# A hand-written order for TensorE and VectorE in the first attention, matmuls of ones before it, and an earlier small load

## The chip, the cores and the metric

One core of one Trainium2 chip runs the whole kernel. The metric is the device time of one execution in microseconds; the profile's span, from the first to the last instruction, is a little shorter. Engines are named as the profile names them: PE (matmul), PEld (its weight loads), DVE (vector), ACT (scalar), POOL (GpSimd), SP (the queue that issues most transfers).

## The reference

The input is x (2 sequences of 1024 rows, 256 wide) and a context (2 x 77 x 192). Everything is float32. Four layers follow each other, each with a residual:

```
x = x + attn0(LN(x), ctx)     # 16 heads of 16, 77 keys, softmax per head
x = x + ffn0(LN(x))           # t + relu(t w1 + b1) w2 + b2, then LN(gamma, beta); t = LN(x)
x = x + attn1(LN(x), ctx)     # one head of 256, own layer norms
x = x + ffn1(LN(x))           # row s uses the matrix W[idx[s]] of 8; idx = argmax(pe @ sign(sigs))
```

In ffn0 the router's weights are replaced by one for expert 0, so only w1[0] and w2[0] count. idx depends on the position alone and is computed from the tile signatures, a table of 8 x 32.

## The kernel before, in words

The 2048 rows are cut into 8 chunks (c) of 256 rows; a chunk has two blocks (b = 2c and 2c + 1) of 128 rows. Each chunk passes attention0, ffn0, attention1 and then to_slots, which sorts its rows by tile into a buffer in device memory, from which block() reads them sorted, or, for the last chunk, by_every_tile.

The code is written as Python generators. Each piece of work is begun with a place, a number on a common scale, and each `yield` gives the place of its next step; `run` (line 159) takes steps from a heap by place and emits their instructions. So places give a program order. From this a planner makes the order on each engine: by default it may advance an instruction whose inputs it expects to be ready. With `manual_schedule(engines=...)` the instructions emitted inside keep their program order on the engines named. Before the change this holds for DVE in steps with a place below 0 (line 874); everything after it (line 875) and all other engines are left to the planner:

```
    run(0, {mybir.EngineType.DVE})
    run(math.inf)
```

Semaphores and buffers are assigned by the framework. Each engine takes its own instructions in the order that results.

The work around the change:
- Loads (lines 93 to 117). SP issues most of them, ACT issues x_0 and wq. Those after `late = True` (line 103) are issued after the first chunk's xT copy ("a0"). The signatures sigT are the 19th load, near the end, on SP.
- first_context (299): the context is transposed (ps_cxT, line 268, copied by DVE, 275) and projected to keys (ps_k, 288); DVE writes them masked by head into kbd (305).
- attention0 (568): moments on DVE (187, 189) and POOL (196, 197); normed on ACT (227), transposed on PE (254), copied by ACT (257); queries ps_q (580) with bias on ACT (585).
- attention0_block (591): scores sc (599), 16 matmuls into the one buffer of four PSUM banks; for each half g a row maximum mx (608) and a subtraction (610) on DVE and an exponential on ACT (614); sums per head (617), reciprocal (621), spread over the head's width on ACT (623: sme); 12 transposes in three banks (634), each copied by ACT (635): ten of the probabilities and, in the third bank, two of sme; weighted values ps_o (643), times the reciprocal on DVE (650: oT); output ps_y (656), added to x by DVE (657). One generator writes these in that order, with pauses before the sums, the transposes, ps_o and ps_y.
- values (327): ps_v (332), copied by ACT (336), spread by five products (341), masked by DVE into vbd (321); then transfers to v_rows for sequence 1.
- row_of_biases (362): bvb on DVE (365), ps_bv (368), added to a row (369), which POOL adds to x (566).
- ffn0 (659): moments, normed, transposed, eight hidden tiles of 128 in four steps (ps_h, 676), two outputs (ps_eo, 688).
- choices (452) computes idx and reads sigT in DVE (455, 456); second_context (375) prepares attention1.

All other matmul results share four PSUM banks (tag "bank").

Of the kernel before, what the change touches and what calls it, by code (L numbers as in the profile page):

```python
# [35 lines left out]
P = 128  # L36
# [27 lines left out]
def tile_blocks(ctx: ExitStack, tc: tile.TileContext, a: dict, out: bass.AP):  # L64
# [12 lines left out]
    def load(name, shape, src, eng=nc.sync, tag=None, bufs=None):  # L77

        if tag is None:
            t = const.tile(shape, F32, tag=name, name=name)  # L80
        else:
            t = work.tile(shape, F32, tag=tag, name=name, bufs=bufs)
        i = eng.dma_start(t, src)
        if late:
            loads.append(i.ins)
        return t
# [9 lines left out]
    cols = load("cols", [P, N_COL], a["cols"])  # L96
    wk = load("wk", [CK, 2, D], rows_of(a["wk"], CK), tag="blk", bufs=6)
    wq = load("wq", [P, KC, D], rows_of(a["wq"]), nc.scalar)
    wv = load("wv", [CK, 2, D], rows_of(a["wv"], CK), tag="blk", bufs=6)
    xs.append(load("x_1", [P, NI, D], x_in[1]))  # L100
    wo = load("wo", [P, KC, D], rows_of(a["wo"]))
# [8 lines left out]
    wv1 = load("wv1", [CK, 2, D], rows_of(a["wv1"], CK), tag="both", bufs=4)  # L110
    wqT = load("wqT", [P, KC, D], rows_of(a["wqT"]), tag="both", bufs=4)
    wo1 = load("wo1", [P, KC, D], rows_of(a["wo1"]), tag="both", bufs=4)
    sigT = load("sigT", [NP, NT], a["sigT"])
    peT = [
        load(f"peT_{s}", [NP, S // 2], a["peT"][:, s * S // 2 : (s + 1) * S // 2], tag="blk", bufs=6)
        for s in range(2)
# [2 lines left out]
    def col(i, p=P):  # L119
        return cols[:p, i : i + 1]  # L120
# [171 lines left out]
        return ps  # L292

    kbd = const.tile([P, B, KC, 2, L], F32, tag="kbd", name="kbd")
    first = {}
# [29 lines left out]
    def values():  # L327
        v = work.tile([L, B, D], F32, tag="tb", name="v")
        ps = bank("ps_v").rearrange("p (e d) -> p e d", e=B)
        for e in range(B):  # L330
            for k in range(2):
                nc.tensor.matmul(
                    ps[:L, e, :], first["cxT"][:, k, e * L : (e + 1) * L], wv[:, k, :],
                    start=k == 0, stop=k == 1,
                )
        nc.scalar.copy(v, ps[:L])
        for c in range(NK):
            yield
            ps = bank(f"ps_v_{c}")
            n0 = c * P % L  # L340
            nc.tensor.matmul(
                ps[:, :D], repeat[:, n0 : n0 + P], v[:, 0, :], start=True, stop=True
            )
            masked(0, c, ps[:, :D], nc.vector)
        yield
        none = work.tile([NK * P - G8, D], F32, tag="yT", name="none", bufs=3)
        nc.gpsimd.memset(none, 0.0)
        nc.sync.dma_start(v_rows[G8:, :], none)
        nc.sync.dma_start(
            v_rows[:G8, :].rearrange("(h l) d -> l h d", l=L),  # L350
            v[:, 1, :].unsqueeze(1).to_broadcast([L, 8, D]),
        )
# [7 lines left out]


    def row_of_biases():
        bvb = work.tile([P, KC, P], F32, tag="oT", name="bvb")
        for k in range(KC):
            nc.vector.tensor_scalar(bvb[:, k, :], ones, col(C_BV + k), None, ALU.mult)
        ps = bank("ps_bv")
        for k in range(KC):
            nc.tensor.matmul(ps[:, :D], bvb[:, k, :], wo[:, k, :], start=k == 0, stop=k == KC - 1)
        nc.vector.tensor_tensor(rows[:, R_BO, :], ps[:, :D], rows[:, R_BO, :], ALU.add)
# [198 lines left out]
    def attention0(c, x):  # L568
        e = c * CH // S
        m = moments(x, NI, f"a{c}")  # L570
        yield 2 * c - 1.8
        n = normed(x, NI, D, f"a{c}", m, act=True)
        yield 2 * c - 1.4
        xT = transposed(n, f"a{c}")
        yield 2 * c - 0.7
        qT = work.tile([P, KC, CH], F32, tag="qT", name=f"qT_{c}")
        ps = bank(f"ps_q_{c}").rearrange("p (g t) -> p g t", g=KC)
        for g in range(KC):
            for k in range(KC):
                nc.tensor.matmul(  # L580
                    ps[:, g, :], wq[:, k, g * P : (g + 1) * P], xT[:, k, :],
                    start=k == 0, stop=k == KC - 1,
                )
        for g in range(KC):
            nc.scalar.activation(qT[:, g, :], ps[:, g, :], AF.Identity, bias=col(C_BQ + g))
        for i in range(NI):
            begin(2 * c + i, attention0_block(c, i, e, x, qT))
        yield 2 * c + 1.2
        with_row(x, x, R_BO)

    def attention0_block(c, i, e, x, qT):
        b = c * NI + i
        pr = prs[b % len(prs)]
        sm = work.tile([P, KC * 8], F32, tag="sm", name=f"sm_{b}", bufs=3)
        sc = ps2.tile([P, 4, 512], F32, tag="sc", name=f"sc_{b}")
        for g in range(KC):
            for j in range(4):
                quarter = slice(j * 32, j * 32 + 32)
                nc.tensor.matmul(  # L599
                    sc[:, j, g * 2 * L : (g + 1) * 2 * L],  # L600
                    qT[quarter, g, i * P : (i + 1) * P],
                    kbd[quarter, e, g].rearrange("p h l -> p (h l)"),
                    start=True, stop=True,
                )
        for g in range(KC):
            scv = sc[:, :, g * 2 * L : (g + 1) * 2 * L].rearrange("p j (h l) -> p j h l", l=L)
            mx = work.tile([P, 4, 2], F32, tag="mx", name=f"mx_{b}_{g}")
            nc.vector.tensor_reduce(mx, scv, AX.X, ALU.max)  # L608
            p8 = pr[:, g, :G8]
            nc.vector.tensor_tensor(  # L610
                p8.rearrange("p (j h l) -> p j h l", j=4, l=L), scv,
                mx.unsqueeze(3).to_broadcast([P, 4, 2, L]), ALU.subtract,
            )
            nc.scalar.activation(p8, p8, AF.Exp, scale=1.0 / math.sqrt(HD))  # L614
        yield b + 0.5
        for g in range(KC):
            nc.vector.tensor_reduce(  # L617
                sm[:, g * 8 : g * 8 + 8], pr[:, g, :G8].rearrange("p (h l) -> p h l", l=L),
                AX.X, ALU.add,
            )  # L620
        nc.vector.reciprocal(sm, sm)
        sme = work.tile([P, KC, 8, HD], F32, tag="sme", name=f"sme_{b}")
        nc.scalar.copy(
            sme, sm.rearrange("p (g h) -> p g h", g=KC).unsqueeze(3).to_broadcast([P, KC, 8, HD])
        )
        yield b + 0.7

        pT = work.tile([P, 3, 4, P], F32, tag="pT", name=f"pT_{b}")
        srcs = [pr[:, g, n * P : (n + 1) * P] for g in range(KC) for n in range(NK)]
        srcs += [sme[:, g].rearrange("p h d -> p (h d)") for g in range(KC)]  # L630
        for n in range(3):
            ps = bank(f"ps_pT_{b}_{n}")
            for j in range(4):
                nc.tensor.transpose(ps[:, j * P : (j + 1) * P], srcs[4 * n + j], ident)  # L634
            nc.scalar.copy(pT[:, n].rearrange("p j t -> p (j t)"), ps)  # L635
        pTs = pT.rearrange("p n j t -> p (n j) t")
        yield b + 1.1
        ps = bank(f"ps_o_{b}")
        for g in range(KC):
            for m in range(4):  # L640
                n0 = 2 * L * m // P
                for n in (n0, n0 + 1):
                    nc.tensor.matmul(  # L643
                        ps[32 * m : 32 * m + 32, g * P : (g + 1) * P],
                        vbd[:, e, n, g, 32 * m : 32 * m + 32],
                        pTs[:, g * NK + n, :],
                        start=n == n0, stop=n > n0,
                    )
        oT = work.tile([P, KC, P], F32, tag="oT", name=f"oT_{b}")
        nc.vector.tensor_tensor(  # L650
            oT, ps[:, : KC * P].rearrange("p (g t) -> p g t", g=KC), pTs[:, KC * NK :, :], ALU.mult
        )
        yield b + 1.5
        ps = bank(f"ps_y_{b}")
        for g in range(KC):
            nc.tensor.matmul(ps[:, :D], oT[:, g, :], wo[:, g, :], start=g == 0, stop=g == KC - 1)  # L656
        nc.vector.tensor_tensor(x[:, i, :], ps[:, :D], x[:, i, :], ALU.add)

    def ffn0(c, x):
        b = 2 * c  # L660
        m = moments(x, NI, f"f{c}")
        yield b + 2.9
        t = normed(x, NI, D, f"f{c}", m, act=True)
# [182 lines left out]

    for c in range(NC):
        begin(-1.4 if c == 1 else 2 * c - 2, attention0(c, xs[c]))
        begin(2 * c + 2.7, ffn0(c, xs[c]))
        begin(2 * c + 6.1, attention1(c, xs[c]))  # L850
        begin(2 * c + 8.1, (to_slots if c < NC - 1 else by_every_tile)(c, xs[c]))
    begin(-1.95, paced(-1.95, 0.4, first_context()))
    begin(1.1, once(row_of_biases))
    begin(-0.3, paced(-0.3, 0.2, values()))
    begin(5.1, paced(5.1, 0.4, values_by_head()))
    begin(3, once(zeros))
    begin(5, paced(5, 0.4, choices()))
# [13 lines left out]
        after(i.ins, "b1")  # L871

    begin(9, once(load_every))
    run(0, {mybir.EngineType.DVE})
    run(math.inf)


# [97 lines left out]
```

## Time and profile before

| | us |
|---|---|
| median of 3 runs | 336.43 |
| lowest, highest | 335.42, 338.63 |
| the profiled execution | 340.51 |
| its span | 338.4 |

The share of the span in which each engine was busy, in 40 slices of 8.46 us each (a digit is tenths):

```profile
PE   2979789999799899999999999999799996578995
DVE  2278884695459657929757784894346659326343
ACT  2246566535234457365464744645324421212110
DMA  7597299999401302701000100250845687164510
```

PE is below 9 tenths in several early slices, near the tenth slice and in slices 33 to 36. DMA is busy in the first five slices and then again from the sixth on, when the sorted buffer is filled with zeros. A line of the order of work has the start in us, the time of the group in us, the engine, the line of the code, the operation, output<-inputs, shapes and how many; what stands in brackets is the idle time before it and who ended it. A line of waits has the total in us, how many there were and the longest.

### The profile page before, as it was taken

How to read it: one execution, taken by the hardware profiler on the slowest of the kernel's cores; microseconds unless marked ns; L12 is line 12 of the kernel's file. 1: busy time of each engine (PE TensorE's matmuls, PEld its weight loads, DVE VectorE, ACT ScalarE, POOL GpSimd, SP SyncE). 2: the span in 40 equal slices, each digit the busy share in tenths (PEclk: the TensorE clock that was granted, in tenths of full speed). 3: DMA queues.
4: the chain of work that ended last, by engine and by line, in shares of the span. 5: the costliest groups of instructions: out<-in, count | busy, mean ns of one | idle time of the engine just before them, and what ended most of it. 6: DMA issues, size and time to landing. Idle time of an engine off the chain costs nothing.

```text
span 338.4 us, 6080 instructions
## 1 busy us (share of the span) xinstructions
PE 301.8 (89%) x2144; PEld 247.6 (73%) x2144; DVE 211.0 (62%) x624; ACT 141.4 (42%) x309; POOL 130.6 (39%) x183
## 2 busy tenths in 40 slices
PE   2979789999799899999999999999799996578995
PEld 2656568888488678877887888888688885455884
DVE  2278884695459657929757784894346659326343
ACT  2246566535234457365464744645324421212110
POOL 3104560424003458346435512432652716415422
PEclk9999999999899999999999999999999999559999
DMA  7597299999401302701000100250845687164510
GB/s 198 197 334 184 104 241 139 213 158 76 39 0 44 115 13 93 255 32 45 20 2 0 64 0 2 69 182 1 252 133 183 204 253 254 64 186 128 167 34 16
DMA packets 23209, 39.69 MB, mean 117 GB/s; under 512 B 2669, under 2 KB 9354, under 8 KB 23180
## 3 DMA queue, kind: packets, MB, share of 16 engines
q1 hardware_dynamic: 19788, 32.22, 38.3%
q0 software_dynamic: 2848, 6.57, 5.9%
q10 hardware_dynamic: 544, 0.52, 0.5%
q8 instruction: 17, 0.28, 0.4%
q14 instruction: 12, 0.10, 0.1%
HBM read 25.52 MB, written 15.62 MB: 122 GB/s over the span
## 4 chain that ended last, share of the span: by engine, by line
PE 63%; DVE 18%; issue 7%; DMA 4%; POOL 3%; ACT 2%; SPq 1%; POOLq 0%; ACTq 0%
PE ps_eo L688 15%; PE ps_h L676 11%; PE ps_t L809 5%; PE ps_pT L634 4%; PE ps_z L834 4%; PE ps_y L656 4%; DVE mx L608 3%; PE ps_q L580 3%; DVE pr L610 3%; PE ps_o L643 2%; PE ps_s L721 2%; PE sc L599 2%; PE ps_y L746 2%; DMA wt<-in_wrow 2%; DMA wk<-in_wk 2%
## 5 line engine op out<-in xcount | busy, mean ns | idle before, releaser
L676 PE MATMUL ps_h<-xT_f,w 128*128 128x256 f32 x256 | 63.3, 390 | 3.0 <-issue 2.1
L688 PE MATMUL ps_eo<-w,hT 128*128 128x256 f32 x256 | 58.4, 381 | 1.9 <-ACT hT L681 1.9
L676 PEld LDWEIGHTS ps_h<-xT_f,w 128*128 128x128 f32 x256 | 47.0, 192 | 11.6 <-issue 4.5
L688 PEld LDWEIGHTS ps_eo<-w,hT 128*128 128x128 f32 x256 | 47.5, 190 | 8.3 <-ACT hT L681 2.3
L173 POOL DMA_INDIRECT out<-res,blk x28 | 27.4, 980 | 38.1 <-DVE res L814 14.5
L681 ACT ACTIVATE hT<-ps_h,cols 128x256 f32<-128x256 f32 x64 | 27.1, 466 | 30.7 <-PE ps_h L676 30.6
L614 ACT ACTIVATE pr<-pr 128x616 f32<-128x616 f32 x32 | 22.9, 717 | 37.5 <-DVE pr L610 37.5
L608 DVE TENSOR_REDUCE mx<-sc 128x8 f32<-128x616 f32 x32 | 25.2, 788 | 5.3 <-PE sc L599 5.3
L635 ACT COPY pT<-ps_pT 128x512 f32<-128x512 f32 x48 | 25.4, 595 | 6.2 <-PE ps_pT L634 6.2
L750 DVE SCALAR_TENSOR_TENSOR x<-ps_y,sm,x 128x256 f32<-128x256 f32 x16 | 7.1, 479 | 29.7 <-PE ps_y L746 29.7
L617 DVE TENSOR_REDUCE sm<-pr 128x8 f32<-128x616 f32 x32 | 24.6, 781 | 1.4 <-ACT pr L614 1.0
L610 DVE TENSOR_TENSOR pr<-sc,mx 128x616 f32<-128x616 f32 x32 | 25.2, 787 | 0.2
L805 ACT COPY yT<-ps_yT 128x256 f32<-128x256 f32 x28 | 10.4, 371 | 35.2 <-PE ps_yT L803 35.2
L634 PE MATMUL ps_pT<-ident,pr 128*128 128x128 f32 x160 | 21.0, 274 | 3.7 <-ACT pr L614 2.0
L566 POOL TENSOR_TENSOR x<-x,rows 128x512 f32<-128x512 f32 x16 | 21.0, 1321 | 8.3 <-ACT n_a L227 5.4
L634 PEld LDWEIGHTS ps_pT<-ident,pr 128*128 128x128 f32 x160 | 18.1, 141 | 5.9 <-ACT pr L614 2.5
L656 PE MATMUL ps_y<-wo,oT 128*128 128x256 f32 x64 | 17.4, 394 | 4.5 <-DVE oT L650 4.5
L765 POOL TENSOR_TENSOR both<-x,bias 128x256 f32<-128x256 f32 x14 | 9.9, 725 | 24.6 <-DVE x L750 24.5
L643 PE MATMUL ps_o<-pT,vbd 128*32 128x128 f32 x512 | 19.0, 283 | 0.1
L643 PEld LDWEIGHTS ps_o<-pT,vbd 128*32 128x32 f32 x512 | 14.4, 112 | 5.7 <-issue 4.5
L809 PE MATMUL ps_t<-wt,yT 128*128 128x256 f32 x60 | 16.9, 403 | 1.8 <-ACT yT L805 1.3
L173 POOL DMA_INDIRECT slots<-both,to x14 | 14.3, 1019 | 9.2 <-DVE both L232 2.7
(196 smaller groups left out, 545.8 us busy)
## 6 DMA issues: line engine op xcount, KB each, us to landing
blk<-slots SPq DMA_DIRECT2D x28, 256.5 KB
slots<-zero SPq DMA_DIRECT2D x1, 3847.5 KB
wt<-in_wrow SPq DMA_DIRECT2D x15, 256.0 KB
slots<-zero SPq DMA_DIRECT2D x1, 3334.5 KB
w<-in_w SPq DMA_DIRECT2D x2, 1024.0 KB
every<-in_wrow SPq DMA_DIRECT2D x1, 2048.0 KB
wt_w<-in_wrow SPq DMA_DIRECT2D x8, 256.0 KB
x<-in_x SPq DMA_DIRECT2D x7, 256.0 KB
```

Of the source, the lines that this page charges most:

```text
L173: i = nc.gpsimd.indirect_dma_start(out=to, out_offset=bass.IndirectOffsetOnAxis(ap=index, axis=0), in_=rows_in, in_offset=None, bounds_che ...
L608: nc.vector.tensor_reduce(mx, scv, AX.X, ALU.max)
L610: nc.vector.tensor_tensor(p8.rearrange("p (j h l) -> p j h l", j=4, l=L), scv, mx.unsqueeze(3).to_broadcast([P, 4, 2, L]), ALU.subtract,)
L617: nc.vector.tensor_reduce(sm[:, g * 8 : g * 8 + 8], pr[:, g, :G8].rearrange("p (h l) -> p h l", l=L), AX.X, ALU.add,)
L634: nc.tensor.transpose(ps[:, j * P : (j + 1) * P], srcs[4 * n + j], ident)
L635: nc.scalar.copy(pT[:, n].rearrange("p j t -> p (j t)"), ps)
L643: nc.tensor.matmul(ps[32 * m : 32 * m + 32, g * P : (g + 1) * P], vbd[:, e, n, g, 32 * m : 32 * m + 32], pTs[:, g * NK + n, :], start=n == ...
L656: nc.tensor.matmul(ps[:, :D], oT[:, g, :], wo[:, g, :], start=g == 0, stop=g == KC - 1)
L676: nc.tensor.matmul(ps[:, j, :], w1[:, k, (f + j) * P : (f + j + 1) * P], tT[:, k, :], start=k == 0, stop=k == KC - 1,)
L681: nc.scalar.activation(hT[-1][:, j, :], ps[:, j, :], AF.Relu, bias=col(C_B1 + f + j))
L688: nc.tensor.matmul(ps[:, :D], hT[f // 2][:, f % 2, i * P : (i + 1) * P], w2[:, f, :], start=f == 0, stop=f == F // P - 1,)
L809: nc.tensor.matmul(ps[:, :D], yT[:, k * P : (k + 1) * P], w[:, k * D : (k + 1) * D], start=k == 0, stop=k == KC - 1,)
```

## The change

It has these parts:
- sigT is loaded by ACT's queue directly after wq, before the late loads.
- `warm(n)` is new: n products of the 128 x 128 matrix of ones with itself, into a bank that nobody reads. It stands at three places: 7 products ahead of the context's transposes, 5 ahead of ps_k, 2 ahead of ps_q.
- `run(1, {PE, DVE})` takes the place of `run(0, {DVE})`: PE and DVE keep program order for all steps with a place below 1.
- Places are written anew for chunk 0's and chunk 1's attention0 and for blocks 0 and 1 (the table FIRST), so that block 1's scores, chunk 1's queries, the values and the bias row stand between the steps of block 0. All steps of blocks 0 and 1 lie below place 1.
- In attention0_block the transposes are cut into three steps: the first two banks come before the sums, the third, with sme, after them. The instructions are the same.
- values starts at 0.02, not -0.3; its spreading products stand at 0.2 and its transfers at 0.9. row_of_biases has its DVE part at -0.7 and its matmuls at 0.25, not both at 1.1. The bias row is added to x of chunk 0 at 0.26, not at 1.2.
- ffn0 of chunk 0 begins at 1.5, not 2.7, and its later steps move by as much.

```diff
@@ loads @@
     wq = load("wq", [P, KC, D], rows_of(a["wq"]), nc.scalar)
+    sigT = load("sigT", [NP, NT], a["sigT"], nc.scalar)
...
-    sigT = load("sigT", [NP, NT], a["sigT"])
...
+    def warm(n):
+        ps = bank(f"warm_{next(number)}")
+        for _ in range(n):
+            nc.tensor.matmul(ps[:, :P], ones, ones, start=True, stop=True)
...
@@ values @@
         for c in range(NK):
-            yield
+            yield 0.2
...
-        yield
+        yield 0.9
...
@@ row_of_biases @@
+        yield -0.7
         bvb = work.tile([P, KC, P], F32, tag="oT", name="bvb")
...
+        yield 0.25
         ps = bank("ps_bv")
...
@@ attention0 @@
         m = moments(x, NI, f"a{c}")
-        yield 2 * c - 1.8
+        at = {1: (-0.65, 0.04, 0.13)}.get(c) or (2 * c - 1.8, 2 * c - 1.4, 2 * c - 0.7)
+        yield at[0]
         n = normed(x, NI, D, f"a{c}", m, act=True)
-        yield 2 * c - 1.4
+        yield at[1]
         xT = transposed(n, f"a{c}")
-        yield 2 * c - 0.7
+        yield at[2]
...
-            begin(2 * c + i, attention0_block(c, i, e, x, qT))
-        yield 2 * c + 1.2
+            begin({1: 0.12}.get(2 * c + i, 2 * c + i), attention0_block(c, i, e, x, qT))
+        yield 2 * c + 1.2 if c else 0.26
         with_row(x, x, R_BO)
+    FIRST = {0: (0.1, 0.14, 0.3, 0.32, 0.34, 0.44), 1: (0.36, 0.37, 0.4, 0.42, 0.46, 0.5)}
@@ attention0_block @@
+        at = FIRST.get(b) or (b + 0.45, b + 0.45, b + 0.5, b + 0.7, b + 1.1, b + 1.5)
...
+        def pT_bank(n):
+            ps = bank(f"ps_pT_{b}_{n}")
+            for j in range(4):
+                nc.tensor.transpose(ps[:, j * P : (j + 1) * P], srcs[4 * n + j], ident)
+            nc.scalar.copy(pT[:, n].rearrange("p j t -> p (j t)"), ps)
+
+        yield at[0]
+        pT_bank(0)
+        yield at[1]
+        pT_bank(1)
+        yield at[2]
         for g in range(KC):
             nc.vector.tensor_reduce(
...
-        yield b + 0.7
...
+        yield at[3]
         srcs += [sme[:, g].rearrange("p h d -> p (h d)") for g in range(KC)]
...
+        pT_bank(2)
-        yield b + 1.1
+        yield at[4]
...
-        yield b + 1.5
+        yield at[5]
...
@@ ffn0 @@
-        b = 2 * c
+        b = 2 * c if c else -1.2
...
@@ the steps @@
-        begin(2 * c + 2.7, ffn0(c, xs[c]))
+        begin(2 * c + 2.7 if c else 1.5, ffn0(c, xs[c]))
...
-    begin(1.1, once(row_of_biases))
-    begin(-0.3, paced(-0.3, 0.2, values()))
+    for place, n in ((-1.96, 7), (-1.56, 5), (-1.39, 2)):
+        begin(place, once(warm, n))
+    begin(-0.7, row_of_biases())
+    begin(0.02, values())
...
-    run(0, {mybir.EngineType.DVE})
+    run(1, {mybir.EngineType.PE, mybir.EngineType.DVE})
     run(math.inf)
```

More of the change, by code (lines that the diff above doesn't have):

```diff
@@ L614, in attention0_block @@
             nc.scalar.activation(p8, p8, AF.Exp, scale=1.0 / math.sqrt(HD))
-        yield b + 0.5
+        pT = work.tile([P, 3, 4, P], F32, tag="pT", name=f"pT_{b}")
+        srcs = [pr[:, g, n * P : (n + 1) * P] for g in range(KC) for n in range(NK)]
+        def pT_bank(n):
[8 more added lines that the diff above has]
+        yield at[2]
         for g in range(KC):
@@ L625, in attention0_block @@
         )
-        yield b + 0.7
-        pT = work.tile([P, 3, 4, P], F32, tag="pT", name=f"pT_{b}")
-        srcs = [pr[:, g, n * P : (n + 1) * P] for g in range(KC) for n in range(NK)]
+        yield at[3]
         srcs += [sme[:, g].rearrange("p h d -> p (h d)") for g in range(KC)]
[L631 to L635, printed above, removed]
+        pT_bank(2)
         pTs = pT.rearrange("p n j t -> p (n j) t")
-        yield b + 1.1
+        yield at[4]
         ps = bank(f"ps_o_{b}")
```

## The prediction

> **What bounds the kernel now.** I read the page's first part, then busy time by stretches, then the order of work in the first 49 us, then the waits of PE and DVE there. All numbers are of the one profiled execution, span 338.4 us.
>
> The busy shares first:
>
> ```profile
> PE 301.8 (89%) x2144; PEld 247.6 (73%) x2144; DVE 211.0 (62%) x624; ACT 141.4 (42%) x309; POOL 130.6 (39%) x183
> ```
>
> Over the whole, PE (matmuls) is nearly the bound: 36.6 us of its span are idle. Where that idle time lies decides. Busy time by stretches (start:end, length, then PE, PEld, DVE, ACT, POOL):
>
> ```profile
> 0.00:13.00 13.00, 6.17 (x21) 5.18 (x22) 4.38 (x18) 2.97 (x5) 4.18 (x21) 1.00 0.58 159
> 13.00:19.00 6.00, 5.70 (x30) 3.52 (x28) 0.42 (x1) 2.50 (x5) 0.00 (x0) 1.00 1.00 326
> 19.00:30.00 11.00, 8.91 (x82) 6.38 (x81) 9.08 (x19) 5.61 (x10) 0.92 (x2) 1.00 1.08 303
> 30.00:41.00 11.00, 8.45 (x87) 6.59 (x86) 10.93 (x29) 5.91 (x12) 7.19 (x10) 1.00 0.28 93
> ```
>
> The reader is to see two regimes. From 13 to 19 us DVE has 0.42 us of work in 6: it waits for the first scores. From 19 to 41 it is busy 20.0 of 22 us: it is the bound until chunk 0 leaves the first attention. From 50 to 85 PE has no idle time at all. So 36.6 us idle splits into about 13 before 50 us and 23.5 after, and the change works on the first part. PE's and DVE's order up to there:
>
> ```profile
> 6.88 2.39 PE L288 MATMUL ps_k<-cxT,wk 96*128 96x154 f32 x8 [2.20 <-DMA wk<-in_wk]
> 9.06 1.06 PE L254 MATMUL ps_xT_a<-ident,n_a 128*128 128x128 f32 x4
> 10.79 3.78 PE L580 MATMUL ps_q<-xT_a,wq 128*128 128x256 f32 x8 [0.68 <-ACT xT_a L257]
> 14.37 2.69 PE L332 MATMUL ps_v<-wv,cxT 96*77 96x256 f32 x8
> 16.99 0.54 PE L599 MATMUL sc<-kbd,qT 32*128 32x154 f32 x6
> ...
> 18.43 0.79 PE L599 MATMUL sc<-kbd,qT 32*128 32x154 f32 x10
> ...
> 19.25 0.80 DVE L608 TENSOR_REDUCE mx<-sc 128x8 f32<-128x616 f32 x1 [0.29 <-PE sc L599]
> ...
> 29.07 1.99 PE L580 MATMUL ps_q<-xT_a,wq 128*128 128x256 f32 x8
> ...
> 39.78 0.41 DVE L657 TENSOR_TENSOR x<-ps_y,x 128x256 f32<-128x256 f32 x1
> ...
> 48.79 1.89 PE L676 MATMUL ps_h<-xT_f,w 128*128 128x256 f32 x8
> ```
>
> Here: the same ps_q costs 3.78 us at 10.79 and 1.99 at 29.07, so PE is cold until about 15.6. The scores of block 0 wait behind ps_v and are split by a ps_v copy, so DVE's first reduction is at 19.25. Block 1 ends at 40.19 (39.78 + 0.41), and the first FFN matmul follows at 48.79. The waits of PE before 50 us:
>
> ```profile
> PE ps_k L288 <- DMA wk<-in_wk: 2.2, 1, 2.2
> PE ps_pT L634 <- ACT pr L614: 2.0, 2, 1.3
> ```
>
> The first is the hole that the five products fill.
>
> [...]
>
> **The change, part by part.**
>
> *Products of ones.* The trace shows four matmuls of projected_T as eight instructions, so 14 products are 28. Nearest row: a 128x128 weight with 77 columns moving, eight in 1.11 us warm (105.34) and 1.99 cold (292.96): 0.14 and 0.25 us each. Seven products then take 14 x 0.25 = 3.5 us, from the end of the memset of ones (1.1) to 4.6. The context landed at 3.96, so its transposes start 0.6 late and end at 5.3 (0.72 cold). DVE's copies (0.53) end at 5.9. Five products: 1.4 us warm to 2.5 cold, ending at 6.7 to 7.8, against wk landed at 6.74. So ps_k is delayed by between 0 and 0.9 us; I take 0.4. With PE busy from 1.1, [...] from ps_k on I count warm. The two last products (0.56) lie beside ACT's copy xT (0.58): nothing.
>
> *The first scores.* ps_k at 7.3, eight warm: 1.05 (ps_wqk, same width, in the chain at 80.40): 8.4. Transposes 0.60 (they took that at 20.54): 9.0. Copy 0.58, hand-over: 9.65. ps_q 1.99: 11.6. Bias on ACT 0.84 (14.61): 12.4. DVE's kbd (1.47) ends near 10, covered. PE now keeps scores ahead of ps_v: 16 in 0.81: 13.2. Before it was 19.21. So DVE begins block 0 **6.0 us** earlier: about 4 from the clock (ps_k 1.3, transposes 0.5, ps_q 1.8), less 0.4, and 2.5 from ps_v being behind.
>
> *The order up to place 1.* DVE from 13.3: two reductions and two subtractions (0.79 each) to 16.5. PE meanwhile ps_v (1.75 warm), transposes of chunk 1, block 0's first transposed bank; scores of block 1 need block 0's PSUM (one buffer), so 17.7: DVE stalls 1.2. Block 1's four operations: 20.9. Masks of the values 5 x 0.42, bias row 0.41: 23.4. Sums of block 0 (2 x 0.79, reciprocal 0.23): 25.3. Now oT_0 stands next in DVE's order, behind sme on ACT (0.41), the third bank (0.44), its copy (0.58) and ps_o (1.12): it can start at 28.1. That hole of 2.8 us is the danger: sums of block 1 stand behind it. The order binds only these steps against each other: in the run before, bvb (place 1.1) ran at 5.29 amid steps ordered by hand, so work of later places can fall in. Block 2's scores (0.81 on PE, 3.2 us on DVE) are ready then: its PSUM is free at 20.9, PE is free from 22.8, its queries are done. I let them fill it: oT_0 at 28.4, sums of block 1 to 30.6, add of block 0 at 31, block 1's ps_o to 33.2, ps_y to 34.9, its add ends at **35.3**, with block 2's scores behind it as before. Before: 40.2. Gain **4.9 us**; 1.1 of the 6.0 are given back to stalls.
>
> *What follows.* FFN of chunk 0 starts at 1.5 in place of 2.7, ahead of blocks 2 and 3. Moments (POOL 0.22 + 0.70), ACT 2 x 0.60, transposes 0.66, copy 0.57: PE gets FFN work near 41, not 48.8, and blocks 2 and 3 become its filler. From there PE is the bound and the 4.9 us stay. The adds on POOL (1.27) start when the bias row is done: 23.5, not 30.6; nobody waits. v_rows' transfers at place 0.9 need only be there for chunk 4: nothing. DMA loads are triggered by the first xT copy, now about 1.1 us earlier; they had landed by 30 (DMA share 1.08 before 30, 0.28 after): nothing. The signatures' issue on ACT (0.5) precedes its first work at 4.59: nothing, but a DVE sign operation drawn forward then finds its data.
>
> *Sum.* 338.4 - 4.9 = 333.5 us span. The execution took 340.5, the median of three is 336.4 (335.4 to 338.6). 336.4 - 4.9 = 331.5; I keep back 0.5 for stalls of the order that I rounded off: **332.0**. Unknown costs: the filling of DVE's hole (from 0.3 better to 3 worse), the clock (0 to 4 us lost of the gain), the planner's order after place 1 (no row shows it; holes of 0.5 to 2 us stand in the trace, such as 2.1 at 89.16; I take plus or minus 2).
>
> **Rivals.** (A) Likeliest: the gain is carried to the end, 328.5 to 334.
>
> (B) It is eaten later. After 85 us PE still has some 20 us of holes, 9 of them from 280 to 300 where DVE is busy 9.33 of 10 and PE waits 4.24 for n_b. If a later transfer or such a chain ends at the same time as before, the time is 335 to 337. For: those waits. Against: 50 to 85 us is full PE, and the late waits are on chunk chains that move along.
>
> (C) Slower: head-of-line waits. If nothing falls into DVE's hole, block 0 and block 1 each cost some 3 us of DVE; or the planner puts matmuls of the second context or the choices into PE's free spots before 30 us, and their weights (issued 18.98 to 25.6) hold the ordered queue for 2 to 5 us. That takes 6 (two holes) to 11 (with the late weights) of a gain of 4.9: plus 1 to plus 6, 337.5 to 342.5. It decides from 5 us of unfilled holes. For: DVE's margin was 2 us in 22. Against: block 2's scores are ready.
>
> (D) The clock doesn't rise: [...] Then ps_k and ps_q stay cold, 4 us go, and only ps_v's move remains: 336.
>
> **Chances.** A 0.56, B 0.13, C 0.26, D 0.05. One per cent, 3.4 us, is what a measurement of this kernel tells from no change: below 333.1 is faster. Of A 0.50 lies below; the rest of A, B, D and 0.09 of C are within; 0.17 of C is above 339.8. Range 328 to 340: it takes in B, D and the nearer end of C, and leaves out about 0.16 of C above and 0.04 of A below.
>
> **What would show it.** Right: ps_q near 9.7 taking 2 us; the first reduction of scores at 13 to 14; block 1's add ending at 35 to 36; ps_h starting near 41. Wrong: a DVE wait for PE of over 2 us before oT_0; PE waiting on wk1, wqT or peT before 30; ps_q still at 3.8; ps_h back at 46 to 49; or new holes after 85 us that add up to the gain.

## The result, and the profile after

| | before | after |
|---|---|---|
| median of 4 runs each, us | 335.93 (335.07 to 338.63) | 345.71 (344.82 to 347.33) |
| the profiled execution, us | 340.51 | 344.82 |
| its span, us | 338.4 | 342.7 |

The ratio is 1.028 [1.021, 1.036]: the change makes the kernel slower by 2.8%, where 332.0 us was forecast, and lies above the range (328 to 340). The traced execution of the kernel before is one of its slower ones, 4.6 us above the median, so the two spans, 4.3 us apart, show less of the loss than the medians, 9.8 us apart.

The start went nearly as forecast. The order of work on PE and DVE in the kernel after (start, us, engine, line, operation, in brackets the idle time before it and its releaser):

```profile
1.16 3.35 PE L298 MATMUL warm<-ones 128*128 128x128 f32 x14 [1.16 <-POOL ones L131]
...
7.41 1.32 PE L288 MATMUL ps_k<-cxT,wk 96*128 96x154 f32 x8 [0.47 <-DVE cxT L275]
...
10.05 2.00 PE L589 MATMUL ps_q<-xT_a,wq 128*128 128x256 f32 x8 [0.23 <-ACT xT_a L257]
...
13.59 0.80 DVE L621 TENSOR_REDUCE mx<-sc 128x8 f32<-128x616 f32 x1 [1.17 <-PE sc L612]
...
37.12 0.41 DVE L677 TENSOR_TENSOR x<-ps_y,x 128x256 f32<-128x256 f32 x1
...
41.42 1.39 PE L254 MATMUL ps_xT_f<-ident,n_f 128*128 128x128 f32 x4 [3.98 <-ACT n_f L227]
43.49 3.78 PE L696 MATMUL ps_h<-xT_f,w 128*128 128x256 f32 x8 [0.67 <-ACT xT_f L257]
```

The first reduction stands at 13.59 (before 19.25), block 1's add ends at 37.53 (before 40.19), the FFN's first matmul is at 43.49 (before 48.79). At that point the changed kernel is **5.3 us ahead**. Two things are seen in the last two lines: PE has been idle for 3.98 us ahead of the FFN's transposes, and it is slower behind the gap: ps_h takes 3.78 us, twice the 1.89 of before, at a granted clock of 0.60 from 41 to 49.

Then the lead turns over. Chunk 1's first ps_h, first before, then after:

```profile
78.51 1.89 PE L676 MATMUL ps_h<-xT_f,w 128*128 128x256 f32 x8
```

```profile
89.09 1.89 PE L696 MATMUL ps_h<-xT_f,w 128*128 128x256 f32 x8
```

The changed kernel is 10.6 us **behind**, so by this mark 15.9 us are lost. Not all of that is left at the end of these two traces: the last stage's ps_z starts at 317.9, before at 313.5, since PE of the kernel before idles 5.5 us between 85 and 160 and that of the changed kernel 1.0. A closer pair of kernels, below, shows the loss undiminished at the end. Busy time by stretches (start:end, length, then PE, PEld, DVE, ACT, POOL with the number of instructions, then the granted clock, the DMA share, GB/s), first before, then after:

```profile
49.00:60.00 11.00, 11.00 (x95) 9.00 (x94) 6.36 (x13) 6.29 (x15) 0.00 (x0) 1.00 1.01 154
60.00:85.00 25.00, 25.00 (x190) 21.84 (x190) 17.55 (x54) 11.62 (x25) 8.58 (x12) 1.00 1.06 143
```

```profile
41.00:49.00 8.00, 6.89 (x25) 5.24 (x26) 3.90 (x8) 5.35 (x12) 5.95 (x7) 0.60 0.00 0
49.00:60.00 11.00, 11.00 (x83) 9.43 (x82) 0.42 (x1) 5.16 (x12) 0.13 (x1) 1.00 0.73 191
60.00:85.00 25.00, 20.79 (x183) 17.33 (x182) 17.99 (x48) 8.63 (x16) 6.33 (x10) 0.86 1.06 176
```

(The kernel before with the products alone, an experiment below traced at 335.28 us, has the same two rows as the kernel before: DVE 6.20 us of 11, then PE 25.00 of 25.) From 49 to 60 PE is busy throughout in both, but DVE does 0.42 us of work, where it did 6.36. After 60 the price is paid: PE, full before, idles 4.2 us of 25 and its clock is down to 0.86. What PE does in that stretch tells why. Its order after 50 us, first before, then after:

```profile
51.92 1.99 PE L676 MATMUL ps_h<-xT_f,w 128*128 128x256 f32 x8
53.84 0.81 PE L599 MATMUL sc<-kbd,qT 32*128 32x154 f32 x16
54.58 1.99 PE L676 MATMUL ps_h<-xT_f,w 128*128 128x256 f32 x8
56.50 1.12 PE L643 MATMUL ps_o<-pT,vbd 128*32 128x128 f32 x32
57.55 1.99 PE L676 MATMUL ps_h<-xT_f,w 128*128 128x256 f32 x8
```

```profile
50.72 3.62 PE L696 MATMUL ps_h<-xT_f,w 128*128 128x256 f32 x16
54.27 1.12 PE L663 MATMUL ps_o<-pT,vbd 128*32 128x128 f32 x32
55.32 2.00 PE L589 MATMUL ps_q<-xT_a,wq 128*128 128x256 f32 x8
57.15 3.62 PE L708 MATMUL ps_eo<-w,hT 128*128 128x256 f32 x16
60.60 1.04 PE L635 MATMUL ps_pT<-ident,pr 128*128 128x128 f32 x8
...
62.78 3.62 PE L708 MATMUL ps_eo<-w,hT 128*128 128x256 f32 x16
66.33 0.81 PE L612 MATMUL sc<-kbd,qT 32*128 32x154 f32 x16
```

Before, the FFN's matmuls come two hidden tiles at a time, with a piece of attention between: block 4's scores at 53.84, a block's ps_o at 56.50. After, they come in long runs, and the scores that feed DVE next come at 66.33, behind all of them. DVE's waits in the first 60 us and PE's over the whole (total, how many, longest):

```profile
DVE oT L670 <- PE ps_o L663: 8.7, 2, 7.9
```

```profile
PE ps_pT L635 <- ACT pr L627: 5.6, 6, 4.2
...
PE ps_xT_f L254 <- ACT n_f L227: 4.0, 1, 4.0
```

DVE stands for 7.9 us before oT of block 2 (then 4.84 more for ps_eo), because ps_o is behind four ps_h. When the scores come at last, DVE is in the norm at the FFN's end and begins their reductions at 69.80; PE has run out of other work by then and waits 4.2 us, until 72.39, for the exponentials that follow them:

```profile
55.54 0.42 DVE L670 TENSOR_TENSOR oT<-ps_o,pT 128x256 f32<-128x256 f32 x1 [7.89 <-PE ps_o L663]
...
69.80 0.79 DVE L621 TENSOR_REDUCE mx<-sc 128x8 f32<-128x616 f32 x1
...
72.39 1.33 PE L635 MATMUL ps_pT<-ident,pr 128*128 128x128 f32 x5 [4.21 <-ACT pr L627]
```

### The profile page after: what moved, and what is told of

Read it like the earlier page. It is cut to its first block, busy times and chain, and to the rows that moved or that the text cites. A ratio compares the mean times of both kernels' runs of the same rounds, so it can differ in the third digit from the quotient of the medians.

```text
span 342.7 us, 6119 instructions
## 1 busy us (share of the span) xinstructions
PE 308.5 (90%) x2172; PEld 254.4 (74%) x2172; DVE 211.5 (62%) x624; ACT 141.2 (41%) x309; POOL 130.3 (38%) x183
## 4 chain that ended last, share of the span: by engine, by line
PE 71%; DVE 15%; DMA 6%; ACT 3%; issue 2%; POOL 2%; ACTq 0%; POOLq 0%; DVEq 0%
PE ps_eo L708 16%; PE ps_h L696 12%; PE ps_t L829 6%; PE ps_pT L635 6%; PE ps_q L589 4%; PE ps_z L854 4%; PE ps_y L676 4%; PE ps_o L663 3%; DVE pr L623 3%; PE sc L612 3%; DVE mx L621 3%; PE ps_y L766 2%; PE ps_s L741 2%; DMA blk<-slots 2%; DMA wt<-in_wrow 2%
## 5 line engine op out<-in xcount | busy, mean ns | idle before, releaser
L696 PEld LDWEIGHTS ps_h<-xT_f,w 128*128 128x128 f32 x256 | 47.8, 195 | 8.5 <-issue 1.6
L636 ACT COPY pT<-ps_pT 128x512 f32<-128x512 f32 x48 | 26.9, 588 | 12.9 <-PE ps_pT L635 12.8
L635 PE MATMUL ps_pT<-ident,pr 128*128 128x128 f32 x160 | 26.1, 293 | 5.6 <-ACT pr L627 5.6
L635 PEld LDWEIGHTS ps_pT<-ident,pr 128*128 128x128 f32 x160 | 20.4, 151 | 9.6 <-ACT pr L627 7.1
L196 POOL TENSOR_SCALAR rs_g<-mv_g 128x2 f32<-128x2 f32 x6 | 1.6, 267 | 49.7 <-DVE mv_g L189 49.7
L712 DVE TENSOR_TENSOR tb<-ps_eo,tb 128x256 f32<-128x256 f32 x16 | 6.7, 422 | 21.3 <-PE ps_eo L708 21.3
L612 PE MATMUL sc<-kbd,qT 32*128 32x154 f32 x256 | 17.6, 327 | 1.6 <-DVE pr L623 1.1
```

Source lines behind the costliest of these rows:

```text
L612: nc.tensor.matmul(sc[:, j, g * 2 * L : (g + 1) * 2 * L], qT[quarter, g, i * P : (i + 1) * P], kbd[quarter, e, g].rearrange("p h l -> p (h ...
L696: nc.tensor.matmul(ps[:, j, :], w1[:, k, (f + j) * P : (f + j + 1) * P], tT[:, k, :], start=k == 0, stop=k == KC - 1,)
```

## The experiments

Each ratio is to the kernel before, run on the same chip; medians of before lay between 335.9 and 339.5. My theory after the first reading was that FFN's early place costs the time; the rival, that the hand order or its products do. The rest of the section follows what that theory had to give up.

**The FFN's place taken back.** Changed kernel, two lines as before:

```diff
-        b = 2 * c if c else -1.2
+        b = 2 * c
-        begin(2 * c + 2.7 if c else 1.5, ffn0(c, xs[c]))
+        begin(2 * c + 2.7, ffn0(c, xs[c]))
```

> The changed kernel with one part undone: ffn0 of chunk 0 begins at 2.7 again and its steps are at their old places. Theory 1 (the earlier place of this FFN bunches its matmuls ahead of blocks 2 and 3, so that DVE has nothing to do from 49 to 66 us and PE then waits for DVE, twice for 4 us, and falls to the half clock after each): both holes go, the head's lead is kept, 329 to 333 us, DVE busy over 5 us between 49 and 60. Theory 2 (the hand order of PE and DVE up to place 1 itself leaves blocks 2 and 3 behind): the time stays at 343 to 347. Theory 3 (any edit reshuffles the planner's later order by a few per cent, without a cause in this step): anywhere from 335 to 347, with the holes elsewhere.

Measured: 337.77 us, 1.001 [0.998, 1.003]. The loss is gone, so it hangs on this place. But the time is not the 329 to 333 us of theory 1; it lies in the range of theory 3 alone, and the head's gain is gone as well: ps_h starts at 49.68, block 1's add at 41.98. DVE's order in this kernel shows why:

```profile
18.27 0.76 DVE L187 BATCH_NORM_STATS2 st_a<-x 128x6 f32<-128x256 f32 x2 [1.75 <-DMA x<-in_x]
...
20.38 0.16 DVE L222 SCALAR_TENSOR_TENSOR sh_a<-mv_a,rs_a 128x2 f32<-128x2 f32 x1 [1.13 <-POOL rs_a L197]
20.45 0.79 DVE L621 TENSOR_REDUCE mx<-sc 128x8 f32<-128x616 f32 x1
```

The planner drew the moments of chunk 2 into the hand-ordered stretch, ahead of block 1's first reduction, which so comes at 20.45 (17.77 in the changed kernel). They wait 1.75 us for rows that haven't landed and 1.13 for POOL. PE's products of the values then wait 2.91 for ACT, and what follows is slow until about 34 us: four of these products take 2.08 us (1.13 in the changed kernel), ps_o at 31.82 takes 1.96 (1.12 at 38.87), and the granted clock is 0.75 from 19 to 30 and 0.78 from 30 to 41.

**The FFN's place alone.** Kernel before with only these two lines of the change. In it chunk 0's FFN takes block 1's rows before attention's output is added to them.

> The kernel before with that one part alone: ffn0 of chunk 0 at 1.5. Theory 1: the loss without the head's gain, so 345 to 352 us, with DVE nearly idle for some 10 us in the first FFN and PE waiting for DVE after it. Theory 2: near the kernel before, 335 to 338. Theory 3: no clear side.

Measured: 1.030 [1.024, 1.036]. The place alone, with no hand order and no products, costs as much as the whole change. In its trace PE is busy 20.34 of the 25 us from 60 on and waits 4.5 us at once for oT. DVE's thin stretch lies earlier than in the changed kernel and is shorter than the 10 us expected (3.61 us of work in 8 from 41 to 49, 5.67 in the kernel before), as its ps_h starts at 38.40; block 4's scores stand behind both ps_eo here too, at 63.05. The rival isn't needed for the loss.

**Products, and signatures.** Changed kernel without the 14 products (the three begins of `warm` taken out); changed kernel with the load of sigT where it was; kernel before with the 14 products alone:

> The changed kernel without the 14 products of ones. If the products are worth what the head shows (PE at full clock at 7.4 us, some 4 us), this is 3 to 5 us slower than the changed kernel, 348 to 351 us, with ps_q near 3.8 us for eight; all later holes as in the changed kernel. If the lead of the head is absorbed by what follows (the wait of PE for DVE after the first FFN), it is equal to the changed kernel, 345 to 347.

> The changed kernel with the load of the signatures at its old place, late on SP. In the changed kernel DVE waits 1.43 us for this load at 6.8 us, ahead of the copy of the context, and ps_k waits 0.47 us for that copy. With the load late the planner has no reason to place the sign operations there: ps_k starts near 6.9 in place of 7.4, and the whole is 0 to 0.6 us faster, that is equal within the noise, 345 us. If instead DVE's sign operations stay early and wait for the late load, DVE stops for some 15 us and the time is over 355.

> The kernel before with the 14 products of ones alone; order, places and loads as before. PE should be at full clock from ps_k on, so ps_q takes 2 us in place of 3.8 and the first reduction of scores comes at 15 to 16 us in place of 19.25. If a lead in the head is worth its time at the end when the planner's order after it stays that of before (theory 1 on what the head is worth), this is 2 to 4 us faster than the kernel before: 0.988 to 0.994 of it. If a lead in the head is swallowed later whatever the order (rival B of the prediction), it is within 0.997 to 1.003.

Measured: 1.043 [1.037, 1.049] without products, 352.19 us, a little above what was expected; 1.039 [1.033, 1.045] with the late signatures, 350.41 us, where no difference from the changed kernel was expected (its interval, 1.021 to 1.036, meets this one at the edge); 0.994 [0.990, 0.997] for products alone. So products help both kernels. Without them ps_q takes 3.78 us at 11.10 and the first reduction is at 16.92. The signatures were a miss, and the trace names it:

```profile
29.38 0.16 DVE L463 TENSOR_SCALAR neg<-sigT 32x8 f32<-32x8 f32 x1 [3.31 <-DMA sigT<-in_sigT]
```

The planner draws this operation forward to where DVE has no slack, and DVE's queue stands 3.31 us for one kilobyte (the subtraction next in its order, whose row maximum had ended at 26.07, starts at 29.46); the FFN's first ps_h then comes at 47.30, 3.8 us later than in the changed kernel. With the early load the same operation comes at 6.78 and stands 1.43, ahead of the context's copy, for which ps_k waits 0.47.

**The hand order kept, its strangers held out.** To test whether drawn-in work ate the lead of the first experiment, the next kernels take that one and begin chunk 2's attention0 at 0.31, inside the hand order but after the first scores; the second also begins the choices (which read sigT) at 0.95; the third holds chunk 2 with the FFN early as in the change:

```diff
-        begin(-1.4 if c == 1 else 2 * c - 2, attention0(c, xs[c]))
+        begin({1: -1.4, 2: 0.31}.get(c, 2 * c - 2), attention0(c, xs[c]))
-    begin(5, paced(5, 0.4, choices()))
+    begin(0.95, paced(5, 0.4, choices()))
```

> The same without holding the sign operations: DVE waits 1.4 us for sigT ahead of the copy of the context, ps_k starts near 7.3 in place of 6.9. Theory 1: 0 to 0.6 us slower than the kernel with both held, 0.982 to 0.990 of the kernel before. If drawn-forward steps were not what cost the run with only the FFN's place undone, it equals that run, near 1.000.

> The changed kernel with ffn0 of chunk 0 back at 2.7 and two steps put into the hand order so that the planner can't draw them forward: the moments of chunk 2 at 0.31 (they waited 1.75 us on DVE for x_2 in the run with only the FFN's place undone, and cost block 1's scores 2.7 us) and the sign operations at 0.95 (they waited 1.4 us for sigT). Theory 1: block 1's add ends near 37 us, ps_h follows near 42 with no hole of PE over 2 us before it, DVE stays busy, and the head's lead stays: 0.980 to 0.988 of the kernel before. Rival (the lead is swallowed later, by the waits from 280 us on): 0.995 to 1.003 with a good head.

> The changed kernel (FFN of chunk 0 at 1.5) with only the moments of chunk 2 held at 0.31. Theory 1 (the FFN's place is what costs the 3 per cent, by itself): DVE again has nothing to do for 7 us or more after 48, PE waits some 4 us for DVE near 70, and the time is that of the changed kernel, 1.02 to 1.035 of the kernel before. If instead the late moments of chunk 2 (at 35 us in the changed kernel) were the cause, this falls to 0.985 to 1.000.

Measured: 0.990 [0.983, 0.997]; **0.988 [0.985, 0.991]**, 334.16 us against 339.06, faster than both kernels; and with the FFN early 1.026 [1.020, 1.032]. So the hand order brings something once these two are kept out of it, and with chunk 2 held in both the FFN's place still costs 3.6%, 13 us (346.72 against 333.71). This is the closer pair: chunk 1's first ps_h is at 87.77 against 75.54, the last stage's ps_z at 318.9 against 306.5. The 12.2 us lost by the first mark are still lost at the second. The best kernel's stretches, then those of the one with the early FFN:

```profile
49.00:60.00 11.00, 11.00 (x96) 9.08 (x95) 6.22 (x11) 6.29 (x14) 0.90 (x2) 1.00 0.99 145
60.00:85.00 25.00, 25.00 (x198) 21.00 (x197) 16.62 (x51) 10.04 (x21) 7.68 (x11) 1.00 1.07 139
```

```profile
49.00:60.00 11.00, 11.00 (x85) 9.44 (x84) 0.59 (x2) 4.33 (x10) 0.00 (x0) 1.00 0.84 198
60.00:85.00 25.00, 20.79 (x186) 17.26 (x185) 18.30 (x48) 9.42 (x18) 6.34 (x10) 0.86 1.07 172
```

It is the pattern of before and after once more: DVE 6.22 or 0.59 us of 11, then PE full or with 4.2 us of holes.

**What of it is needed.** The best kernel without PE in the hand order (`run(1, {DVE})`), and without products:

> The kernel with both steps held, but only DVE keeps its order up to place 1; PE's order is the planner's, which again puts half of ps_v ahead of block 0's scores. If PE's order by hand is worth what the forecast gave it (ps_v behind the scores, some 1 us warm), 0.990 to 0.995; if nothing, 0.985 to 0.990; if the hand order costs by its head waits, under 0.985.

> The kernel with both steps held, without the 14 products. The head is then cold (ps_q 3.8 us). If the lead comes from the clock in the main, 0.997 to 1.005; if the order alone brings it, under 0.992.

Measured: 0.987 [0.982, 0.993] and 0.988 [0.980, 0.996]. Holding PE's order adds nothing to holding DVE's that these intervals can show. The second is a miss: without products the FFN starts 2.1 us later (48.17 against 46.03), and yet the last stage's ps_z starts at 308.67, with them at 308.78. Head gains don't add up: those of the products were not to be seen at the end here, though they were in the changed kernel.

**Which half of the FFN's place.** In the best kernel, its moments, norm and transposes early (begun at 1.5) and the matmuls where they were; then the other way round (ps_h earlier by 0.25, ps_eo by 1.2):

```diff
-        yield b + 2.9
+        yield b + 2.9 if c else 1.7
-        yield b + 3.2
+        yield b + 3.2 if c else 2.0
```

```diff
-            yield b + 3.5 + 0.13 * f
+            yield (b if c else -0.25) + 3.5 + 0.13 * f
-            yield b + 4.6 + 0.5 * i
+            yield (b if c else -1.2) + 4.6 + 0.5 * i
```

> The kernel with both steps held (0.988 of the kernel before), but with the FFN of chunk 0 begun at 1.5 for its moments, normalization and transposes only; its matmuls stay at their old places. If the matmuls' places are what costs (PE does both outputs of the FFN before it gives DVE the scores of block 4), this stays at 0.983 to 0.995. If the early normalization costs (it pushes chunk 2's normalization and queries behind on POOL and ACT), this rises to 1.015 to 1.03.

> The kernel with both steps held, but with the FFN's matmuls of chunk 0 early (hidden tiles by 0.25, outputs by 1.2, so that both outputs stand together ahead of block 2's ps_o); its moments, normalization and transposes stay at the old places. If the matmuls' places cost: 1.005 to 1.03, with DVE waiting some 5 to 9 us for ps_o or ps_eo between 50 and 70. If the early normalization costs: 0.983 to 0.995.

Measured: 0.996 [0.993, 1.000] and 0.992 [0.988, 0.997], so 0.9% and 0.5% over the best kernel, the latter within the intervals, and both far from 3.6. The first is telling, for it has the idle PE that I had suspected:

```profile
PE ps_xT_f L254 <- ACT n_f L227: 3.9, 1, 3.9
```

PE's gap of 3.9 us is there in full, with a granted clock of 0.74 from 30 to 41, and most of the loss isn't: PE is busy 25.00 of 25 from 60 on, and chunk 1's first ps_h is at 80.18, 4.3 us later than in the best kernel (75.84). In its order, the queries of chunk 2 stand ahead of the first ps_h and block 4's scores behind the second pair. So the gap can account for 0.9 of the 3.6%, and neither half makes the rest alone.

**The attention beside it.** So three kernels change the neighbours, all with chunk 2's moments held. One leaves the FFN early and puts chunk 2's queries ahead of ps_h and block 4's scores ahead of ps_eo. One leaves the FFN where it was in the best kernel and delays the same work until it is behind ps_eo. One leaves the FFN early and moves blocks 2 to 5 and chunk 2's queries along by the same 1.2:

```diff
+        at = {1: ..., 2: (1.65, 1.9, 2.05)}.get(c) or ...
+            begin({1: 0.12, 4: 3.3, 5: 3.95}.get(...), attention0_block(...))
```

```diff
+        at = {1: ..., 2: (2.2, 2.6, 3.95)}.get(c) or ...
+            begin({1: 0.12, 4: 5.2, 5: 5.3}.get(...), attention0_block(...))
```

```diff
+        at = {1: ..., 2: (1.0, 1.4, 2.1)}.get(c) or ...
+            begin({1: 0.12, 2: 1.0, 3: 1.8, 4: 2.8, 5: 3.8}.get(...), attention0_block(...))
+        p = b - 1.2 if b in (2, 3, 4, 5) else b
+        at = FIRST.get(b) or (p + 0.45, p + 0.45, p + 0.5, p + 0.7, p + 1.1, p + 1.5)
```

> The changed kernel with the FFN of chunk 0 still at its early place, chunk 2's moments in the written order, and two of its steps put back ahead of the FFN on PE: chunk 2's queries stand before the first ps_h, block 4's scores before the first ps_eo (in the changed kernel both stand behind all of the FFN's matmuls they could stand ahead of). Theory (the early FFN costs time only because it pushes block 4's scores behind its 14 us of matmuls, and DVE then has no attention left to do): DVE's busy time from 49 to 60 us returns from 0.6 to 4 us or more, its wait of 9 us for ps_o goes below 5, and the ratio to the kernel before is 0.985 to 1.00. Rival (the early FFN costs by itself, through the gap that PE has before it and the cold clock after, and the scores have no part in it): 1.015 to 1.03 as with the early FFN and the scores behind it, 1.026.

> The best kernel so far (0.9877) with its FFN of chunk 0 where it was, and chunk 2's queries and block 4's and 5's scores begun later, so that block 4's scores stand behind the last ps_eo of the FFN, as they do in the changed kernel. Theory (it is the late scores that cost): DVE starves somewhere between 50 and 66 us, with one wait of 5 us or more for PE there that the best kernel hasn't, PE waits for pr or oT after it, and the ratio to the kernel before is 1.01 to 1.03, though the FFN isn't early at all. Rival (the early FFN itself costs): 0.985 to 0.995, as the best kernel.

> The changed kernel with chunk 0's FFN still at its early place 1.5, and all that stood beside it moved along by the same 1.2: the steps of blocks 2 to 5 and of chunk 2's queries. So the FFN has its early place, but on PE its matmuls have the attention of blocks 2 to 4 between them again, as in the kernel before. Theory (the early place costs because attention falls behind the FFN as a block; scores of block 4 alone, put back, gave 1.0109, since the ends of blocks 2 and 3 stayed behind): chunk 1's first ps_h near 76 us, not 87 to 89, no DVE wait of 5 us between 48 and 66 us, and a ratio to the kernel before of 0.985 to 1.00. Rival (an early FFN costs whatever stands beside it): 1.01 to 1.03, chunk 1's first ps_h after 84.

Measured: 1.011 [1.000, 1.022], **1.028 [1.019, 1.036]** and 1.008 [1.005, 1.011].

The second is the clearest: the FFN isn't early at all, block 4's scores start at 66.76, behind the last ps_eo, and the best kernel (0.988) becomes as slow as the changed one. Its stretches and the waits of DVE from 40 to 70 us:

```profile
49.00:60.00 11.00, 11.00 (x83) 9.36 (x82) 1.52 (x5) 5.38 (x14) 0.00 (x0) 1.00 1.00 142
60.00:85.00 25.00, 19.39 (x141) 15.36 (x139) 14.67 (x40) 7.51 (x16) 7.63 (x11) 0.86 1.05 140
```

```profile
DVE oT L670 <- PE ps_o L663: 7.2, 1, 7.2
```

DVE starved first (1.52 us of 11), PE with holes (19.39 us of 25) and a granted clock of 0.86 after: the changed kernel's picture without its early FFN.

So late scores are enough to cost as much. The first says that block 4's scores are not all of it. They are at 55.48 now, but block 2's ps_o still stands behind four ps_h, DVE still waits 7.6 us for it, and block 3's ps_y still comes only at 71.86 (59.38 before). The ratio, 1.011, lies between the ranges of the theory (up to 1.00) and the rival (from 1.015), and that wait, which the theory put below 5 us, is still above it. The third puts the whole order beside the FFN back. Up to 65 us its order on PE is nearly that of the best kernel (block 4's scores at 49.54, there 50.34), DVE's wait of over 5 us is gone and its busy time from 49 to 60 is 5.61 us. About half of the 3.6% goes (1.026 to 1.008, where 0.990 has the FFN at its old place). That is between the two ranges again, and chunk 1's first ps_h, which the theory put near 76 and the rival after 84, is at 84.21. Its trace has a second, smaller hump: from 60 to 85 PE is busy 21.04 us, with waits of 2.16 and 1.40 us at 71.91 and 73.74. Blocks 4 and 5 had been moved along, while chunk 1's FFN and the second context, which stand beside them, had not. I read it as the same fault one chunk on; no run shows that. That late attention is the whole cost of the early FFN isn't shown either.

One figure divides all the kernels of this case: PE is busy 24.4 us or more of the 25 from 60 on in those at 0.987 to 1.001, and 21.04 or less in those from 1.008 up. It doesn't set the size of the loss (21.04 at 1.008, 20.80 at 1.043). It speaks against theory 3 of the first experiment, that any edit reshuffles the planner's later order with no cause in this step; no run tests that theory by itself.

## Why the prediction was wrong, by its own steps

- **The head** was right in kind and near in size: ps_k at 7.41 (7.3 forecast), ps_q at 10.05 with 2.00 us (9.65, 1.99), the first reduction at 13.59 (13.3). PE was at full speed for ps_q, as forecast; that a PE busy from 1.1 us would bring this was my estimate, and without the products ps_q took 3.78.
- **The order up to place 1.** DVE's hole was filled by block 2's reductions, as argued, and oT of block 0 came at 29.16 (28.4), after a wait of 0.80 us. Block 1's add ended at 37.53, not 35.3: PE had waited 1.69 us for sme, was granted 0.86 of the clock from 19 to 30 us, and ps_o took 1.96 us where 1.12 was used. Of 4.9 us forecast, 2.7 were there.
- **"PE gets FFN work near 41"** held for the transposes, 41.42, but the first ps_h came at 43.49. The gap of 3.98 us ahead of the transposes, and the halved speed of the first ps_h (3.78 us, later 1.89), were not forecast.
- **The step that failed** is the next: "blocks 2 and 3 become its filler. From there PE is the bound and the 4.9 us stay." Blocks 2 and 3 were not filler. The ends of their attention and the scores of block 4 fell behind the FFN's matmuls, DVE ran dry, and after 60 us DVE's work came too late for PE. Its term in the sum, the planner's order after place 1 at plus or minus 2 us, was the one mis-sized: 15.9 us went between 43 and 89, and the FFN's place measured by itself costs 13 us (346.72 against 333.71). None of the signs of being wrong that the prediction names appeared; the hole came between 60 and 85, where it looked for none.
- I read a full PE from 50 to 85 us in the profile of before as proof that PE is the bound there whatever its order. It was full because attention and FFN were interleaved; its idle time was hidden in that order, not absent.
- **The signatures** were priced at nothing, an estimate that no trace had shown, with the note that a drawn-forward operation then finds its data. It stood 1.43 us on DVE for them. Without the early load it stands 3.31 at a worse place, so the part seems worth having in this kernel.
- **The rivals.** C was named for the right kind of cause, head-of-line waits, and its range (337.5 to 342.5) was nearest. But its place, before 30 us, and its holes were others: DVE had no wait of over 2 us for PE ahead of oT. That its range was nearest is luck. B, a gain eaten later, describes the first experiment in part, where it was eaten at 18 us rather than after 85. D did not come (ps_q took 2.00 us).
- **Two figures of the working.** The clock's part of the first 6.0 us is called about 4, but its terms (1.3, 0.5, 1.8) add up to 3.6. DVE's 9.33 us of 10 belong to 280 to 290 alone; from 290 to 300 it is busy 1.85. Neither touches the step that failed.

## What to carry to other kernels

A full engine in a profile is not yet a bound (here PE's 25.00 us of 25 became 20.79): ask what keeps it full. Where one engine's work is the filler of another's waits, moving a long piece of it forward pushes the short pieces behind it that a second engine lives on, and the price is paid later, when that engine has become the bound. If a planner may draw work into a hand-written stretch, give the likely candidates places of their own; here that turned a change worth nothing (1.001) into one worth 1.2% (0.988).

## What the runs showed of the hardware

- After two gaps of about 4 us in the changed kernel PE ran at half speed: eight ps_h took 3.78 us after 3.98 of idle PE (1.89 at 48.12), and four ps_y 1.91 us behind the wait of 4.21 at 72.39 (1.03 at 61.48).
- Shorter gaps did the same here. In the first experiment, after 2.91 us of idle PE, four products of the values took 2.08 us (1.13 in the changed kernel). In the changed kernel, after 1.69 us at 26.66, ps_o took 1.96 us (1.12 at 34.09) and the granted clock was 0.50 from 27 to 30. Yet a gap of 1.72 us in the kernel before, at 38.51, left four ps_y at 1.13. What decides between these is not shown.
- The column of the granted clock doesn't show the slow start: it reads 1.00 from 0 to 13 us in the kernel before, where ps_q took 3.78 us (1.99 at 29.07). The durations do.
- Here a load of one kilobyte was no faster than the large ones ahead of it: sigT, third in ACT's queue behind two loads of 256 KB, was issued at 1.70 us and took 5.1 to land, they 3.6 and 4.5; DVE waited for it until 6.78.
